# A windowed-attention stage: the mask in the scores' 64x64 tiling, and the weights' transposes, the values and the values' copy moved within a step

## The chip, the cores and the metric

The kernel runs on one core of a Trainium2 chip. The metric is device time in microseconds (us) for one execution. Before the change it is 1746.39 us, the median of 3 runs (1744.85 to 1749.19).

Five engines work side by side, each through its own instructions in order: PE (TensorE, the matrix unit; its weight loads are listed as PEld), DVE (VectorE), ACT (ScalarE), POOL (GpSimd) and SP (SyncE, here only a queue of transfers). They wait for each other by semaphores.

## The reference

Four stages run on 8 sequences of 512 tokens of 128 features, each followed by a layer norm. The change is in the last of them, two layers of windowed attention with a gated feed-forward part:

```
def _layer(x, wqkv, qs, ksc, wo, lg, lb, w1, b1, w2, b2):
    h = shift_token(x)                       # half of the features come from the token before
    q, k, v = split(h @ wqkv, 3)             # 8 heads of 64
    q = l2norm(q) * qs;  k = l2norm(k) * ksc
    q, k = rotary_xpos(q, k)
    # windows of 64 queries against 128 keys: their own window and the one before
    sim = einsum('bhwid,bhwjd->bhwij', q * 8, k)
    mask = (i < j) | (i > j + 64) | (j == -1)
    attn = softmax(where(mask, -max, sim))
    x = x + (attn @ v) @ wo
    h = layernorm(shift_token(x)) * lg + lb
    a, g = split(h @ w1 + b1, 2)
    return x + (a * gelu(g)) @ w2 + b2
```

`j == -1` holds for the missing window before a sequence's first.

## The kernel before

The earlier stages (attention with a distance bias, a feed-forward part with quantised operands, a second attention) take the first 1045 us or so: the last stage's scores run from 1046.4 to 1692.5 us of the profiled span, which ends at 1743.2.

The last stage goes through 16 items `k` (8 sequences in layer 0, then 8 in layer 1) of 4 chunks `c` of 128 tokens. A chunk holds two windows, `w` = 0 and 1, and 8 heads as 4 pairs `pr` with a half `s` each: `s` = 0 lies on partitions 0 to 63, `s` = 1 on 64 to 127. The program has a step for each chunk number `t` = 4k + c (the loop at line 1017), and works on several chunks in one step. Four steps make a **round**; c0 to c3 are its steps by the chunk t, so that the scores of a chunk c = 0 stand in step c2. In a step, in the order in which the lines stand:

- `begin` (PE, chunk t): the q and k projections into `q_ps` and `k_ps`, one PSUM bank each.
- `weights_T` (PE, chunk t-4): eight 128x128 transposes of the softmax weights `pw` into `p_ps`.
- `squares` of k (ACT) and `rotate` of q (DVE, two operations with outputs `was_k`, `was_q`).
- `over_sums` (chunk t-3): a reciprocal on DVE, then POOL divides `pw` by the sums.
- `weights_taken` (DVE, chunk t-4): two copies `pT<-p_ps`.
- `scores` (PE, chunk t-2): the mask, as a product of a bf16 selection matrix and a bf16 mask table, starts each of two PSUM banks `sp` (one for each `s`), and 16 products of 64 features, 64 queries and 128 keys are added to them. The pool of `sp` has one buffer for each half.
- `squares` of q (ACT; it follows `rotate` of q, as both read `q_ps`), `maxima` (DVE: two reductions of `sp`, and a small operation `m<-m,was_v`).
- In c3: `load_T` (PE transposes `hT`, ACT copies them). In c2: `turned` (PE transposes `nT` of an earlier item's normalised tokens), `turned_taken` (ACT copies `nT`), `v_of`, and `geglu`: six products `gp`, `ap`, three Gelu activations on ACT, three operations `u` on DVE. In c1: `normed` (DVE statistics of `hn`, POOL's small operations on them).
- `rotate` of k (DVE), `v_of` (PE: `v_ps`, ACT: a copy `v`, SP: two transfers into `ve`), `operands_T` (PE: eight transposes into `t_ps`), `operands` (ACT: copies `kT` and `qT`).
- `values` (PE, chunk t-4): 32 products of 64 columns, `o_ps<-pT,v` and `o_ps<-pT,ve`.
- `sizes` (DVE: a reduction `was_v<-was_k` and an addition; POOL: an addition).
- `weights` (ACT, chunk t-2): eight Exp activations `pw<-sp,m`, each with a read of its sum.
- `norms` (POOL: a maximum, a power of 2.93 us, a product `was_k<-was_k,was_v`).
- `values_taken` (ACT, chunk t-4): a copy `oT<-o_ps`. In c1 `normalized` (four ACT operations on `hn`) follows.
- `sums` (PE `y_ps`, DVE two additions into `xs`): output projection of chunk t-5 and second feed-forward product of chunk t-11.

Every engine executes in exactly this order of lines. Other than `q_ps`, `k_ps` and `sp`, products go to four PSUM banks in turn. Almost all instructions go through a helper at line 646, so the profile names line 646 for them; they are told apart by the tile.

The scores' mask before:

```
for s in range(2):
    r = slice(64 * s, 64 * s + 64)
    by, to = (twice[r], mask[r, 1]) if c else (identb, mask[:, 0])
    mm(sp[s], lhsT=by, rhs=to, start=True, stop=False, skip_group_check=True)
```

So for c = 0 it multiplies 128 rows by 128 columns, for the others 64 by 128, while the scores that follow use 64 by 64 and the values 128 by 64 parts of PE's array.

Of the kernel before, what the change touches and what calls it, by code (L numbers as in the profile page):

```python
# [11 lines left out]
BF16 = mybir.dt.bfloat16  # L12
I32 = mybir.dt.int32
AF = mybir.ActivationFunctionType
ALU = mybir.AluOpType
# [3 lines left out]
P = 128  # L19
# [6 lines left out]
C_ID, C_TRI, C_SEL, C_MASK0, C_MASK, C_ROT = 0, 128, 256, 512, 640, 768  # L26
# [25 lines left out]
def body(ctx, tc, x, consts, rows, wa0, wa1, acols, bo, wf, wqkv, wo, w1, w2, cols, b2r, qs, ks, out):  # L52
    nc = tc.nc
# [10 lines left out]
    sel = outer.tile([P, 2 * P], BF16, name="sel")  # L64
# [577 lines left out]
    def ffn1():  # L642
# [4 lines left out]
        mm, tr, act, copy = kept(nc.tensor.matmul), kept(nc.tensor.transpose), kept(nc.scalar.activation), kept(nc.scalar.copy)  # L647
# [53 lines left out]
        def shifted(src, h):  # L701

            p_set(h[0:1, 0, 64:128], 0.0)
            for at, n in ((0, 112), (112, 15)):
                nc.sync.dma_start(out=h[at + 1 : at + 1 + n, :, 64:128], in_=src[at : at + n, :, 64:128])
            nc.sync.dma_start(out=h[0:1, 1:NT, 64:128], in_=src[P - 1 : P, 0 : NT - 1, 64:128])
            nc.sync.dma_start(out=h[:, :, 0:64], in_=src[:, :, 0:64])
            return h

        def rows_of(k):  # L710
            return slice((k % B) * NT, (k % B + 1) * NT)
# [36 lines left out]
        def load(k):  # L748
            item[k]["h"] = shifted((xs if k >= B else xn)[:, rows_of(k), :], hq)
# [32 lines left out]
        def main():  # L782
            with ExitStack() as st:
                pool = lambda name, bufs, **k: st.enter_context(tc.tile_pool(name=f"l{name}", bufs=bufs, **k))
                const = pool("c", 1)
# [2 lines left out]
                tiles = lambda t: t.rearrange("p (c d) -> p c d", c=NT)  # L788
                identb = const.tile([P, P], BF16, name="identb")
                nc.vector.tensor_copy(identb, ident)  # L790
                twice = const.tile([P, P], BF16, name="twice")
                nc.vector.tensor_tensor(twice, sel[:, 0:P], sel[:, P : 2 * P], ALU.add)
                mask = const.tile([P, 2, 4, P], BF16, name="mask")
                for i, at in enumerate((C_MASK0, C_MASK)):
                    nc.vector.tensor_copy(mask[:, i], cst[:, at : at + P].unsqueeze(1).broadcast_to([P, 4, P]))
# [1 line left out]
                for i in range(2):  # L797
                    t = const.tile([P, 4, PAD + S], F32, name=f"kT{i}")
# [38 lines left out]
                def scores(k, c, h):  # L837


                    kT, qT = kTs[k % 2], h.pop("qT")  # L840
                    h["sp"] = sp = [p_s.tile([P, 4, P], F32, tag=f"s{s}", name="sp") for s in range(2)]
                    for s in range(2):
                        r = slice(64 * s, 64 * s + 64)
                        by, to = (twice[r], mask[r, 1]) if c else (identb, mask[:, 0])
                        mm(sp[s], lhsT=by, rhs=to, start=True, stop=False, skip_group_check=True)
                    for pr in range(4):
                        for s in range(2):
                            r = slice(64 * s, 64 * s + 64)
                            for w in range(2):
                                at = c * P + 64 * w  # L850
                                mm(
                                    sp[s][64 * w : 64 * w + 64, pr, :], lhsT=qT[r, pr, 64 * w : 64 * w + 64],
                                    rhs=kT[r, pr, at : at + P], start=False, stop=pr == 3 and w == 1, skip_group_check=True,
                                )
# [118 lines left out]
                def turned(k):  # L973
                    item[k]["nT_ps"], hn = bank("nT"), item[k].pop("hn")
                    for c in range(NT):
                        tr(item[k]["nT_ps"][:, c * P : (c + 1) * P], hn[:, c, :], ident)
# [26 lines left out]
                def load_T(k):  # L1003
                    item[k]["hT"] = transposed(item[k].pop("h"), "hT", 3)

                def at_(j, f, *a):
                    if 0 <= j < LAST:
                        f(*divmod(j, NT), chunk[j], *a)

                def begun(t, f, *a):  # L1010
                    if t >= EARLY:
                        at_(t, f, *a)
# [4 lines left out]
                for t in range(1, LAST):  # L1017
                    k, c = divmod(t, NT)
                    if c == 1 and k + 1 < K:
                        load(k + 1)  # L1020
                    begun(t, begin)
                    at_(t - 4, weights_T)
                    begun(t, squares, 1)
                    begun(t, rotate, 0)
                    at_(t - 3, over_sums)
                    at_(t - 4, weights_taken)
                    at_(t - 2, scores)
                    begun(t, squares, 0)
                    at_(t - 2, maxima)
                    if c == 3 and k + 1 < K:  # L1030
                        load_T(k + 1)
                    if c == 2 and 0 <= k - 2 < K:
                        turned(k - 2)
                        turned_taken(k - 2)
                        at_(t - 2, v_of)
                        geglu(k - 2)
                    if c == 1 and 0 <= k - 2 < K:
                        normed(k - 2)
                    begun(t, rotate, 1)
                    if not (c == 2 and 0 <= k - 2 < K):  # L1040
                        at_(t - 2, v_of)
                    at_(t - 1, operands_T)
                    at_(t - 1, operands)
                    at_(t - 4, values)
                    begun(t, sizes)
                    at_(t - 2, weights)
                    begun(t, norms)
                    at_(t - 4, values_taken)
                    if c == 1 and 0 <= k - 2 < K:
                        h = item[k - 2]["hn"]  # L1050
                        normalized(h, h, item[k - 2].pop("shape"))
                    sums(t - 5, t - 11)
                    if c == 0 and 0 <= k - 2 < K:
                        hn = work.tile([P, NT, D], F32, tag="hn", name="hn", bufs=1)
                        item[k - 2]["hn"] = shifted(xs[:, rows_of(k - 2), :], hn)
                    if t in (4, 5):
                        scaled_weights(t - 4)
                    if t == 6:
                        tables(1)
                    z = t - 11  # L1060
                    if z >= B * NT and z % NT == NT - 1:
                        item[z // NT]["shape"] = moments(xs[:, rows_of(z // NT), :], "f")
                    if z > B * NT and z % NT == 0:
                        finished(z // NT - 1 - B)
# [168 lines left out]
def _constants():  # L1233
    p, f = np.arange(P)[:, None], np.arange(P)[None, :]
    c = np.zeros((P, C_ALL), np.float32)
    c[:, C_ID : C_ID + P] = p == f
    i = p % 64
    c[:, C_TRI : C_TRI + 64] = -2.0 * np.maximum(f[:, 0:64] - i, 0)
    c[:, C_TRI + 64 : C_TRI + P] = -2.0 * np.maximum(i - f[:, 0:64], 0)
    for a in range(2):  # L1240
        c[:, C_SEL + a * P : C_SEL + (a + 1) * P] = f == 64 * a + i
    seen = (f >= i) & (f <= i + 64)
    c[:, C_MASK : C_MASK + P] = np.where(seen, 0.0, -1e30)
    c[:, C_MASK0 : C_MASK0 + P] = np.where(seen & ((p >= 64) | (f >= 64)), 0.0, -1e30)
    half = np.arange(0, DH, 2, dtype=np.float32)
    inv_freq = np.float32(1.0) / np.float32(10000.0) ** (half / np.float32(DH))
    t = np.arange(S, dtype=np.float32)
    freqs = (t[:, None] * inv_freq[None, :]).astype(np.float64)
    base = (half + np.float32(0.4 * DH)) / np.float32(1.4 * DH)
    power = (t - S // 2) / np.float32(32.0)  # L1250
    scale = base.astype(np.float64)[None, :] ** power.astype(np.float64)[:, None]
    cos, sin = np.cos(freqs), np.sin(freqs)
    for n, sc in enumerate((8.0 * scale, 1.0 / scale)):
        for k, (a, z) in enumerate(((cos, cos), (-sin, sin))):
            tab = np.concatenate([a * sc, z * sc], 1).reshape(NT, P, DH).transpose(1, 0, 2)
            at = C_ROT + (2 * n + k) * NT * DH
            c[:, at : at + NT * DH] = tab.reshape(P, NT * DH)

    at, blk = np.arange(S) - S // 2, np.arange(S) // 64
    rows = np.zeros((17, 2, S), np.float32)  # L1260
    for n in range(8):
        sign = np.where(blk <= n, 1.0, -1.0)
        rows[n, 0], rows[8 + n, 0] = blk == n, (blk == n) * at
        rows[n, 1], rows[8 + n, 1] = sign * at, -sign
    rows[16, 1] = -1.0
    return c, rows
# [55 lines left out]
```

## Time and profile before

| what | value |
|---|---|
| time, median of 3 runs | 1746.39 us (1744.85 to 1749.19) |
| profiled execution: span, first to last instruction | 1743.2 us |
| granted TensorE clock over the span | 0.972 |
| busy, share of the span: PE / DVE / ACT / POOL | 94% / 80% / 72% / 52% |
| a round of layer 0 (1309 to 1350), of 41 us: PE / DVE / ACT / POOL busy | 41.00 / 34.91 / 33.75 / 34.10 |
| a round of layer 1 (1599 to 1641), of 42 us: the same | 41.56 / 37.05 / 35.28 / 37.03 |
| one Exp of the last stage, mean, x512 | 479 ns |
| two pT copies, DVE, mean of one | 666 ns |

The median lies 3.2 us over the profiled span; a time is compared with the one, a row of the trace with the other. PE's spans in the trace contain the way through the array, so that one matmul's span overlaps the next: what it costs is read from the distance of two starts. The last stage's weight is in its rounds: FFN products (`gp`) begin in 14 steps of the loop, from 1121.8 us on, and the last two items' come after the loop.

### The profile page before, as it was taken

How to read it: one execution, taken by the hardware profiler on the slowest of the kernel's cores; microseconds unless marked ns; L12 is line 12 of the kernel's file. 1: busy time of each engine (PE TensorE's matmuls, PEld its weight loads, DVE VectorE, ACT ScalarE, POOL GpSimd, SP SyncE). 2: the span in 40 equal slices, each digit the busy share in tenths (PEclk: the TensorE clock that was granted, in tenths of full speed). 3: DMA queues.
4: the chain of work that ended last, by engine and by line, in shares of the span. 5: the costliest groups of instructions: out<-in, count | busy, mean ns of one | idle time of the engine just before them, and what ended most of it. 6: DMA issues, size and time to landing. Idle time of an engine off the chain costs nothing.

```text
span 1743.2 us, 42096 instructions
## 1 busy us (share of the span) xinstructions
PE 1638.7 (94%) x16305; PEld 947.9 (54%) x16305; DVE 1387.7 (80%) x2220; ACT 1257.6 (72%) x2996; POOL 911.8 (52%) x974
## 2 busy tenths in 40 slices
PE   3999999999988889999999988999999999999995
PEld 2454555455546644444444436566766676666664
DVE  4688777878839888888888857888888888888873
ACT  0577777777764558877777867788887888888883
POOL 3223332332125741323322157988888888888873
PEclk7899999999998979999999999999999999999998
DMA  6635222221110234233223101111111111111110
GB/s 133 143 72 142 65 54 47 68 58 26 14 14 1 62 78 81 64 63 74 67 49 59 42 4 35 35 35 37 41 38 35 35 41 37 43 42 42 37 35 25
DMA packets 92809, 90.27 MB, mean 52 GB/s; under 512 B 45969, under 2 KB 58257, under 8 KB 92610
## 3 DMA queue, kind: packets, MB, share of 16 engines
q1 hardware_dynamic: 87280, 85.52, 22.8%
q8 instruction: 130, 2.13, 0.5%
q10 hardware_dynamic: 1234, 1.52, 0.3%
q0 software_dynamic: 4096, 0.54, 0.2%
q14 instruction: 69, 0.57, 0.1%
HBM read 41.85 MB, written 18.87 MB: 35 GB/s over the span
## 4 chain that ended last, share of the span: by engine, by line
PE 75%; DVE 8%; ACT 6%; POOL 5%; issue 2%; DMA 2%; SPq 1%; DVEq 0%; ACTq 0%; POOLq 0%
PE av L259 15%; PE s_ps L259 12%; PE t_ps L259 9%; PE y_ps L646 5%; PE sp L646 4%; PE o_ps L646 3%; PE t_ps L646 3%; PE v_ps L646 3%; ACT e L48 2%; PE q_ps L646 2%; PE k_ps L646 2%; PE p_ps L646 2%; PE gp L646 2%; PE ap L646 2%; PE o_ps L260 2%
## 5 line engine op out<-in xcount | busy, mean ns | idle before, releaser
L48 DVE TENSOR_REDUCE m<-s_ps 128x2 f32<-128x1024 f32 x512 | 621.3, 1224 | 150.4 <-PE s_ps L259 146.1
L48 ACT ACTIVATE e<-t_ps 128x512 f32<-128x512 f32 x1024 | 556.1, 596 | 179.9 <-PE t_ps L259 173.1
L259 PE MATMUL av<-e,va 128*32 128x256 f32 x4096 | 328.3, 393 | 10.7 <-ACT avs L48 10.6
L259 PE MATMUL s_ps<-k,q 63*128 63x512 f32 x1024 | 263.1, 509 | 24.1 <-DMA q<-far 17.7
L48 POOL DMA_DIRECT2D q<-mt x128 | 68.9, 542 | 361.2 <-ACT mt L48 361.2
L259 PE MATMUL t_ps<-q,k 64*128 64x512 f32 x1024 | 247.6, 447 | 1.3 <-ACT e L48 1.3
L646 ACT ACTIVATE pw<-sp,m,was_v 128x128 f32<-128x128 f32 x512 | 227.3, 479 | 1.5 <-DVE m L646 1.0
L259 PEld LDWEIGHTS s_ps<-k,q 63*128 63x128 f32 x1024 | 98.6, 188 | 230.5 <-issue 154.0
L646 POOL TENSOR_TENSOR was_v<-was_v 128x16 f32<-128x16 f32 x64 | 187.5, 2930 | 5.3
L259 PEld LDWEIGHTS av<-e,va 128*32 128x32 f32 x4096 | 81.5, 108 | 100.8 <-issue 59.3
L259 PEld LDWEIGHTS t_ps<-q,k 64*128 64x128 f32 x1024 | 121.9, 189 | 23.3 <-ACT e L48 11.3
L646 POOL TENSOR_TENSOR pw<-pw,den 128x1024 f32<-128x1024 f32 x64 | 121.2, 1894 | 7.6 <-DVE den L646 7.6
L646 ACT ACTIVATION_READ_ACCUMULATOR pw<-sp,m,was_v 128x1 f32 x512 | 116.0, 227 | 0.0
L259 PEld LDWEIGHTS <-sel 64*128 64x128 bf16 x2048 | 66.5, 97 | 76.3 <-issue 53.5
L646 DVE TENSOR_REDUCE m<-sp 128x4 f32<-128x512 f32 x128 | 82.3, 684 | 18.9 <-PE sp L646 17.2
L646 POOL TENSOR_TENSOR was_k<-was_k,was_q 128x512 f32<-128x512 f32 x64 | 88.1, 1376 | 7.8 <-DVE was_q L646 7.8
L48 POOL CAST parts<-x 128x512 fp32r<-128x512 f32 x32 | 19.4, 607 | 135.9 <-ACT x L48 135.9
L646 ACT COPY v<-v_ps 128x512 f32<-128x512 f32 x64 | 37.6, 588 | 71.9 <-PE v_ps L646 71.9
L646 PEld LDWEIGHTS t_ps<-cst,was_k 128*128 128x128 f32 x512 | 59.6, 142 | 44.3 <-issue 22.6
L646 DVE COPY pT<-p_ps 128x512 f32<-128x512 f32 x128 | 79.9, 666 | 0.5 <-PE p_ps L646 0.5
L646 PEld LDWEIGHTS p_ps<-cst,pw 128*128 128x128 f32 x512 | 59.8, 141 | 32.3 <-issue 27.5
L646 DVE TENSOR_REDUCE was_v<-was_k 128x16 f32<-128x1024 f32 x64 | 77.1, 1205 | 0.0
(192 smaller groups left out, 3292.0 us busy)
## 6 DMA issues: line engine op xcount, KB each, us to landing
far<-parts SPq DMA_DIRECT2D x64, 256.0 KB
q<-far SPq DMA_DIRECT2D x256, 64.0 KB
k<-far SPq DMA_DIRECT2D x240, 64.0 KB
ve<-v SPq DMA_DIRECT2D x112, 128.0 KB
xn<-in_x SPq DMA_DIRECT2D x8, 256.0 KB
q<-mt POOLq DMA_DIRECT2D x128, 4.0 KB, 3.1
hn<-xs SPq DMA_DIRECT2D x16, 128.0 KB
hn<-xs SPq DMA_DIRECT2D x16, 112.0 KB
```

The costliest lines, as they stand in the source:

```text
L48: return lambda *a, **k: self.tc.keep_in_program_order(f(*a, **k))
L259: mm = lambda *a, **k: tc.keep_in_program_order(nc.tensor.matmul(*a, **k))
L260: tr = lambda *a, **k: tc.keep_in_program_order(nc.tensor.transpose(*a, **k))
L646: kept = lambda f: lambda *a, **k: tc.keep_in_program_order(f(*a, **k))
```

## The change

Five edits, all in the last stage:

1. The mask is written as four products of 64 by 64 (`s` by `w`), all with the bf16 identity `identb`; the matrix `twice` and the DVE operation that made it go, and the first window's mask table is used for `w` = 0 of c = 0 alone.
2. `weights_T` stands ahead of `begin`.
3. `weights_taken` stands ahead of `rotate` of q (and of `over_sums`).
4. `values` stands directly behind `scores`.
5. `values_taken` stands behind `squares` of q, ahead of `maxima`, `turned_taken`, `v_of`, `operands` and `weights`.

Steps after the loop (`rest`, line 1068) keep their order.

```diff
-                twice = const.tile([P, P], BF16, name="twice")
-                nc.vector.tensor_tensor(twice, sel[:, 0:P], sel[:, P : 2 * P], ALU.add)
...
-                    for s in range(2):
-                        r = slice(64 * s, 64 * s + 64)
-                        by, to = (twice[r], mask[r, 1]) if c else (identb, mask[:, 0])
-                        mm(sp[s], lhsT=by, rhs=to, start=True, stop=False, skip_group_check=True)
+                    for w in range(2):
+                        for s in range(2):
+                            r = slice(64 * s, 64 * s + 64)
+                            mm(
+                                sp[s][64 * w : 64 * w + 64], lhsT=identb[r, r], rhs=mask[r, 1 if c or w else 0],
+                                start=True, stop=False, skip_group_check=True,
+                            )
...
+                    at_(t - 4, weights_T)
                     begun(t, begin)
-                    at_(t - 4, weights_T)
                     begun(t, squares, 1)
+                    at_(t - 4, weights_taken)
                     begun(t, rotate, 0)
                     at_(t - 3, over_sums)
-                    at_(t - 4, weights_taken)
                     at_(t - 2, scores)
+                    at_(t - 4, values)
                     begun(t, squares, 0)
+                    at_(t - 4, values_taken)
                     at_(t - 2, maxima)
...
                     at_(t - 1, operands_T)
                     at_(t - 1, operands)
-                    at_(t - 4, values)
                     begun(t, sizes)
                     at_(t - 2, weights)
                     begun(t, norms)
-                    at_(t - 4, values_taken)
...
-    c[:, C_MASK0 : C_MASK0 + P] = np.where(seen & ((p >= 64) | (f >= 64)), 0.0, -1e30)
+    c[:, C_MASK0 : C_MASK0 + P] = np.where(seen & (f >= 64), 0.0, -1e30)
```

## The prediction

> **What bounds the kernel now.** I read the page's busy shares first, then stretches of the last stage, then the waits, and last the chain and three engines' timelines over a round. By the page and the stretches, PE is full.
>
> ```profile
> PE 1638.7 (94%) x16305; PEld 947.9 (54%) x16305; DVE 1387.7 (80%) x2220; ACT 1257.6 (72%) x2996; POOL 911.8 (52%) x974
> ```
> ```profile
> 1309.00:1350.00 41.00, 41.00 (x427) 28.15 (x423) 34.91 (x67) 33.75 (x99) 34.10 (x29) 1.00 0.17 37
> 1599.00:1641.00 42.00, 41.56 (x427) 28.09 (x428) 37.05 (x76) 35.28 (x104) 37.03 (x34) 1.00 0.15 36
> ```
>
> The columns are PE, PEld, DVE, ACT, POOL. A round of layer 0 has no gap on PE; one of layer 1 has, so something else paces it. The waits (1100 to 1680) name it:
>
> ```profile
> PEld gp L646 <- ACT nT L646: 11.2, 14, 1.1
> ...
> ACT was_k L646 <- DVE was_q L646: 4.3, 14, 0.5
> ```
>
> In c2 of each round PE's `gp` waits for ACT's copy `nT`, and ACT in turn for DVE's `rotate`. The chain in a round of layer 1 is not PE's there:
>
> ```profile
> 1573.47 1.58 DVE was_k L646
> 1575.05 0.40 DVE xs L646 x2
> 1575.45 0.60 DVE was_k L646
> 1576.05 0.61 DVE was_q L646
> 1576.83 0.40 issue
> 1577.23 0.59 ACT nT L646
> 1577.87 1.13 PE gp L646 x2
> ```
>
> How tight the same place is in layer 0: `gp` starts at 1328.25, just when PE is free of `v_ps`, and the `nT` copy ends at 1328.18 (1327.59 + 0.59): some 0.03 us spare after a semaphore. The three timelines there:
>
> ```profile
> 1325.71 0.68 DVE L646 TENSOR_TENSOR was_k<-q_ps,was_q 128x512 f32<-128x512 f32 x1
> 1326.31 0.68 DVE L646 TENSOR_TENSOR was_q<-q_ps,was_q 128x512 f32<-128x512 f32 x1
> 1326.90 0.19 DVE L646 RECIPROCAL den<-den 128x8 f32<-128x8 f32 x1
> 1327.01 1.24 DVE L646 COPY pT<-p_ps 128x512 f32<-128x512 f32 x2
> 1328.17 1.28 DVE L646 TENSOR_REDUCE m<-sp 128x4 f32<-128x512 f32 x2
> ```
> ```profile
> 1324.16 0.64 ACT L646 COPY oT<-o_ps 128x512 f32<-128x512 f32 x1
> 1324.62 1.71 ACT L646 ACTIVATE hn<-hn,mr,rstd 128x128 f32<-128x128 f32 x4
> 1326.17 0.64 ACT L646 ACTIVATE was_k<-k_ps 128x512 f32<-128x512 f32 x1
> 1327.08 0.60 ACT L646 ACTIVATE was_k<-q_ps 128x512 f32<-128x512 f32 x1 [0.26 <-DVE was_q L646]
> 1327.59 0.59 ACT L646 COPY nT<-nT 128x512 f32<-128x512 f32 x1
> ```
> ```profile
> 1309.39 1.90 POOL L646 TENSOR_TENSOR pw<-pw,den 128x1024 f32<-128x1024 f32 x1
> ...
> 1318.61 1.89 POOL L646 TENSOR_TENSOR pw<-pw,den 128x1024 f32<-128x1024 f32 x1
> ```
>
> **The loop.** DVE's small `m` ends 0.02 us after POOL's `pw` wherever the two overlap (1302.26 after 1302.24; 1311.31 after 1311.28; 1320.52 after 1320.49), and takes 0.45 to 0.96 us instead of 0.17. From `m` follow `rotate` of k, the reduction, POOL's power and product, and the next `pw`. So a round is a closed path: from `rotate` of k in c2 (1293.14) to `m` of c3 9.12 us, to `m` of c0 9.04, to `m` of c1 9.22 (1320.52), then statistics, `rotate`, reduction and additions until DVE is free in c2, 5.19 (1325.71), then `rotate` of q, ACT's `squares`, `nT`, `gp` 2.54 (1328.25), then PE's six products and DVE's `u` to `rotate` of k 6.17 (1334.42). Sum 41.28: the round of PE. In layer 1 POOL's row is longer by 1.0, and the round is 42.26: there this loop alone paces.
>
> **The change part by part.** *Mask and values on PE.* Starts in c0: last transpose of `p_ps` 1307.79, mask 1308.00, first score 1308.32, second group 1308.48, then every 0.11. A change of tiling thus costs 0.1 over the streaming (0.21 for 512 columns). With the mask in the scores' tiling 0.11 goes and most of 0.05 (first loads not fetched ahead); the new mask's own loads cost 0 to 0.05, the nearest row being the scores' first group. I take 0.13. A 64x64 bf16 mask is in no row: four scores' products start within 0.02 us and run together, two bf16 masks of 64x128 too, so I take the four as together, 0.21; if they went by pairs 0.43, one by one 0.85. In c2 two masks of 128 rows went in turn (1325.34 to the first score at 1325.86): 0.34 goes behind the first mask, and a drain of 0.1 now stands ahead of it, 0.24. *Values behind scores*: the way from `t_ps` into `o_ps` (0.20 instead of 0.11) and out to `y_ps` (0.16 instead of 0.06, then 0.21 instead of 0.11) goes, and the drain behind the scores is there already: 0.20. PE alone: 0.33 in c0, c1, c3, 0.44 in c2, 1.43 a round.
>
> *What the scores' banks make of it.* The second mask waits for the last Exp of the step before; `o_ps` now lies in this path. Before: mask 1308.00 to `v_ps` 1310.48, three copies and eight Exps to 1315.60, 0.05 to a next mask: 7.65, hidden in a step of 8.72. Now `o_ps` with its drain (1.08) less 0.13 comes in: 8.60 in c0 and c1; c3 with `hT` (0.39) 8.99; c2: mask to the end of `t_ps` 9.02 (1325.34 to 1334.36) plus 1.08 less 0.34, then the table load and Exps to the mask at 1340.19, 5.83: 15.59. Sum 41.78, more than the 41.28 of now: this alone takes all of PE's gain.
>
> *`weights_taken` ahead of `rotate` of q.* In c2 DVE is the late one, free at 1325.71 only while `q_ps` is long done. Two copies, 1.15 us (1327.01 to 1328.17), now precede `rotate`, ACT's `squares` and `nT`: the loop grows by 1.15. In the other steps DVE waits before `maxima` (0.50 for the scores in c0), which covers the move. *`values_taken` ahead of `nT`*: `oT` takes 0.46 of ACT (1324.16 to 1324.62) between `squares` and `nT`: 0.46 more. In c0, c1, c3 it lies in ACT's wait for `v_ps` (2.16 us before 1310.52). `o_ps` waits for `pT` too, some 0.7 us in c2, but is free before ACT is.
>
> *Hidden.* `weights_T` 1.7 us sooner: its `pw` is done at 1311.28 and needed at 1314.0, where the q projection starts now. Banks: its second one waits for the `qT` copy, done at 1312.07, needed at 1314.5. `ve` transfers are issued at 1311.1 to 1312.3 and used two steps on, some 15 us. POOL's and SP's orders stay; no DMA moves. `twice` goes before the stage, 0.1 or less. Tail: 0 to 0.9 more, `o_ps` in one last pass, nothing taken.
>
> **Two rules of the Trainium skill against this.** DVE's copies of `pT` ran beside POOL operations with SBUF inputs (1576.68, during an addition to 1577.43) in 0.63 us, unblocked; `m` was blocked. The page "SBUF — State Buffer", "Who interferes with whom", lets a DVE copy in a two-port mode, and any DVE operation with two SBUF inputs, be locked out by GpSimd. [...] "TensorEngine Tiling (Array Packing)", "Restrictions", says that column tiling switches fast weight load off, so the new mask's loads are slower; no row here shows such a load; the sum, which the loop sets, would stay.
>
> **Sum.** 1.15 + 0.46 = 1.61 a round: 42.9 in layer 0, 43.9 in layer 1; both exceed 41.78, so the banks' path stays hidden. 14 rounds of the loop hold `gp`: 14 x 1.61 = 22.5, less 9 x 0.03 spare, is 22. On the profiled span, 1743.2 to 1765; on the runs, which lie 3.2 above, 1746.4 to 1768.5.
>
> **Rivals.** *PE paces alone* (the other side): then a round loses 1.43 and the wait of 0.30 that c3's second mask has now (1339.89 to 1340.19), 39.55: 9 x 1.73 + 5 x 2.71 = 29, about 1717. For it: PE's 41.00 of 41.00 and the chain of layer 0. Against: `gp` has 0.03 spare, and the scores' banks have one buffer. It decides only if the loop had over 1.6 of room and the last Exp came 0.2 (c0) to 1.6 (c2) sooner. *The banks alone pace*: DVE takes the copies in idle time; layer 0 9 x 0.5 more, layer 1 5 x 0.5 less: 2 more, 1748.5, no change. Against: DVE idles nowhere between 1319.57 and 1328.8. *Half of the shift*: ACT or DVE hides one move: 14 x 0.46 to 14 x 1.15, 1753 to 1763. *The masks do not run together*: one by one adds 0.64 a step to the banks' path, 44.3 a round: 3.0 x 9 + 2.1 x 5 = 37, 1784; by pairs 42.6, hidden. *The change does not do what it says* (a drain remains ahead of the scores): 0.16 a step, 42.4 a round on the banks' path, hidden: the forecast's time.
>
> **How the numbers follow.** Forecast 0.70, half of the shift 0.12, masks apart 0.08, banks alone 0.05, PE alone 0.05. The forecast's own spread is 1761 to 1776 (a tail of 0.9, 0.5 either way a round). The range 1753 to 1784 takes in half of the shift and masks apart and leaves out the two rivals of 0.05. Within 0.3% (5.2 us; finer a measurement of this kernel can't tell) lie the banks alone and a shift that is smaller yet: 0.06; faster 0.05; slower 0.89.
>
> **What would show it.** Rounds of 42.9 and 43.9 instead of 41.28 and 42.26; in c2 `gp` waits for ACT's `nT` some 0.4 us, and `o_ps` for DVE's `pT` 0.7 in layer 0 and 1.5 or so in layer 1; masks wait for ACT's `pw`, mostly in c3, 1.6 where before it was 0.30; the step from mask to first score falls from 0.32 to between 0.21 and 0.26. Wrong I am if rounds get shorter, if `gp` follows `v_ps` at once, or if `m` no longer ends with `pw`.

## The result, and the profile after

| kernel | median, us | lowest to highest | ratio to before, 95% interval |
|---|---|---|---|
| before | 1745.91 | 1744.85 to 1749.19 (4 runs) | |
| after | 1763.12 | 1758.02 to 1765.72 (4 runs) | 1.0096 [1.0078, 1.0113] |

The change costs 17.2 us on the medians. The profiled execution of the changed kernel lies 19.9 above that of before: span 1763.1 against 1743.2, clock 0.970 against 0.972. Forecast were 22 more and 1768.5.

The page's busy shares and the same two stretches of the last stage as before (PE, PEld, DVE, ACT, POOL, then the clock):

```profile
PE 1633.9 (93%) x16433; PEld 958.8 (54%) x16433; DVE 1382.8 (78%) x2219; ACT 1263.1 (72%) x2996; POOL 912.1 (52%) x974
```
```profile
1309.00:1350.00 41.00, 39.23 (x430) 27.94 (x430) 33.68 (x64) 32.25 (x92) 33.06 (x27) 1.00 0.17 37
1599.00:1641.00 42.00, 40.57 (x437) 28.78 (x436) 35.13 (x75) 35.77 (x104) 36.96 (x34) 1.00 0.18 43
```

PE was full in layer 0 (41.00 of 41.00). Now 1.8 us of the stretch are empty, and every other engine does less in that stretch too: the same work lies in a longer round. In layer 1 PE has only 1.0 less than before. What PE waits for, between 1100 and 1680:

```profile
ACT was_k L646 <- DVE was_q L646: 21.9, 27, 1.5
...
PE sp L646 <- ACT pw L646: 16.8, 16, 1.4
PEld gp L646 <- ACT nT L646: 13.2, 13, 1.1
...
PEld o_ps L646 <- DVE pT L646: 7.1, 18, 0.6
```

The row of `sp` was 0.6 us before, in one wait; now it is 16.8 in 16. The row of ACT behind `rotate` of q went from 4.3 to 21.9. The chain through c2 of a round in layer 0:

```profile
1337.76 1.20 DVE pT L646 x2
1338.95 0.60 DVE was_k L646
1339.55 0.61 DVE was_q L646
1340.16 0.02 issue
1340.18 0.02 ACTq L646
1340.20 0.04 issue
1340.24 0.58 ACT was_k L646
1340.82 0.38 issue
1341.20 0.61 ACT nT L646
1341.82 0.04 issue
1341.86 1.12 PE gp L646 x2
```

The two moved copies stand in the chain ahead of `rotate`. The 0.38 called issue between `squares` and `nT` is the other moved piece, `oT`, as ACT's own timeline shows:

```profile
1340.24 0.60 ACT L646 ACTIVATE was_k<-q_ps 128x512 f32<-128x512 f32 x1 [1.23 <-DVE was_q L646]
1340.74 0.58 ACT L646 COPY oT<-o_ps 128x512 f32<-128x512 f32 x1
1341.20 0.60 ACT L646 COPY nT<-nT 128x512 f32<-128x512 f32 x1
```

From the starts of `gp`, the whole difference of the two profiled executions can be told round by round:

| stretch | before | after | difference | forecast |
|---|---|---|---|---|
| to the last stage's first mask | 1045.39 | 1046.30 | +0.9 | 0 |
| first mask to first `gp` | 76.43 | 78.80 | +2.4 | +1.6 |
| second round | 41.30 | 44.75 | +3.4 | +1.6 |
| 7 rounds of layer 0, mean | 41.28 | 42.98 | +11.9 | +11.3 |
| the round between the layers | 41.29 | 42.95 | +1.7 | +1.6 |
| 4 rounds of layer 1, mean | 42.27 | 41.90 | -1.5 | +6.4 |
| last of these `gp` to the end | 80.74 | 81.82 | +1.1 | 0 to 0.9 |

So layer 0 is what was forecast (42.94 to 42.96 in six of the seven rounds), layer 1 went the other way, and the start lost more. The first and the last row are no effect of a step that can be named: over the 14 profiled executions of this study the first mask starts anywhere from 1043.6 to 1048.0, and the tail takes 80.4 to 83.7.

### The profile page after: what moved, and what is told of

Same layout as the page of the kernel before. It is cut to its first block, busy times and chain, and to the rows that moved or that the text cites. A ratio compares the mean times of both kernels' runs of the same rounds, so it can differ in the third digit from the quotient of the medians.

```text
span 1763.1 us, 42324 instructions
## 1 busy us (share of the span) xinstructions
PE 1633.9 (93%) x16433; PEld 958.8 (54%) x16433; DVE 1382.8 (78%) x2219; ACT 1263.1 (72%) x2996; POOL 912.1 (52%) x974
## 4 chain that ended last, share of the span: by engine, by line
PE 68%; DVE 11%; ACT 8%; POOL 5%; issue 3%; DMA 3%; SPq 1%; DVEq 0%; ACTq 0%; POOLq 0%
PE av L259 15%; PE s_ps L259 12%; PE t_ps L259 9%; PE y_ps L646 4%; PE sp L646 3%; PE gp L646 2%; ACT e L48 2%; DVE was_k L646 2%; PE ap L646 2%; ACT pw L646 2%; PE o_ps L646 2%; PE o_ps L260 2%; PE p_ps L646 2%; PE t_ps L646 2%; PE q_ps L646 2%
## 5 line engine op out<-in xcount | busy, mean ns | idle before, releaser
L646 DVE SCALAR_TENSOR_TENSOR u<-ap,cols_s,u 128x512 f32<-128x512 f32 (+3 forms) x51 | 36.6, 717 | 67.2 <-ACT u L646 35.5
L646 PE MATMUL sp<-kT,qT 64*64 64x128 f32 x2048 | 80.3, 271 | 0.5 <-ACT qT L646 0.5
L646 PE MATMUL o_ps<-pT,ve 128*64 128x64 f32 x1024 | 71.4, 230 | 6.5 <-DVE pT L646 5.9
```

The source lines that it names most:

```text
L646: kept = lambda f: lambda *a, **k: tc.keep_in_program_order(f(*a, **k))
```

## The experiments

Unless said otherwise a round is the distance of two `gp` groups in the profiled execution. All ratios are to the kernel before, timed beside the run.

### Which move costs what

**1. `over_sums` behind `maxima`**, in the changed kernel, so that POOL's `pw` can't start before `m` is done.

```diff
-                    at_(t - 3, over_sums)
                     at_(t - 2, scores)
...
                     at_(t - 2, maxima)
+                    at_(t - 3, over_sums)
```

> The changed kernel with over_sums (DVE's reciprocal, POOL's division pw) placed behind maxima instead of ahead of scores, so that DVE's m no longer stands behind POOL's pw. Theory A (in layer 0 the loop of DVE, POOL and ACT sets the round of 42.95, because m ends with pw): m takes 0.17 us in every step, the loop opens, and every round falls to the path through the scores' banks, 41.78: 8 rounds of layer 0 by 1.17, some 9 us less than the changed kernel, about 1754. Rival B (what costs is DVE's amount of work in c2, or PE's waits for the moved copies): rounds stay at 42.9, 1763. Rival C (PE's own work sets the pace once m is free): rounds of 39.6 to 41.0, below 1746.

Measured: 1757.70 us (1753.32 to 1761.97), ratio 1.0066 [1.0048, 1.0083]. `m` takes 0.17 us in every step of the rounds. Four of seven rounds of layer 0 are 41.77, the banks' path, the other three 43.2 to 43.8; layer 1 has 41.75 in three of four. So the loop went through `m`, and behind it the banks stand at 41.77. The long rounds have a new limit: DVE's statistics wait for the transfer of `hn` (`DVE bn <- DMA hn<-xs`, 7.8 us in 5 waits). The later `pw` moves the blocking: POOL's product `was_k<-was_k,was_q` behind it now runs beside `rotate`'s last operation on k, of the same name on DVE, which takes 1.62 us instead of 0.68 (from 1322.63, while POOL's runs from 1322.43 to 1323.69). So the additions into `xs`, which the transfer reads, come later.

**2. `weights_taken` behind `rotate` of q again**, all else as changed.

```diff
-                    at_(t - 4, weights_taken)
                     begun(t, rotate, 0)
                     at_(t - 3, over_sums)
+                    at_(t - 4, weights_taken)
```

> The changed kernel with weights_taken back behind rotate of q and over_sums. Theory A (the longest way from DVE's end of c1 to gp counts): now o_ps waits for pT, which ends 2.56 us after DVE is free, and nT, v_ps follow on PE: gp 5.0 us after DVE is free instead of 4.2, so rounds of layer 0 grow by 0.8 to 0.9, 7 us more, about 1770; layer 1 the same or up to 0.3 a round more. Rival B (the copies' 1.15 us ahead of rotate is the cost, whatever stands where): rounds of layer 0 fall by 1.15 to 41.8, about 1754.

Measured: 1782.05 us (1779.20 to 1782.90), ratio 1.0200 [1.0184, 1.0217]: undoing this edit makes it worse. Layer 0 has 43.76, as the first theory had it. Layer 1, which that theory left within 0.3 us, has 44.7 to 44.8 in three of four rounds: `m` of c1 starts 0.37 us behind `pw` there and takes 1.55, so that the loop is closed again. Experiment 9 shows the reason for layer 0 without the other edits.

**3. `values_taken` behind `turned_taken`** in the steps c2 that have `geglu`, so that ACT copies `nT` first.

```diff
                     begun(t, squares, 0)
-                    at_(t - 4, values_taken)
+                    if not (c == 2 and 0 <= k - 2 < K):
+                        at_(t - 4, values_taken)
                     at_(t - 2, maxima)
...
                         turned_taken(k - 2)
+                        at_(t - 4, values_taken)
```

> The changed kernel, in the steps c2 with geglu alone values_taken placed behind turned_taken, so that ACT copies nT before oT. Theory A (ACT's oT lies in the loop with 0.46 us): gp then waits for PE's own v_ps, 0.42 us sooner: layer 0 42.5 a round, 8 times 0.42, 3.4 us less, about 1760; layer 1 unchanged. Rival B (the banks' path alone sets the round, or oT is hidden): no change, 1763.

Measured: 1757.28 us (1749.61 to 1760.09), ratio 1.0058 [1.0038, 1.0077]. Layer 0 has 42.50, 0.45 less than the changed kernel (the term was 0.46), layer 1 41.75. The copy of `oT` is a link of layer 0's loop. Its size is read from the changed kernel, 0.46 us from the start of `oT` to that of `nT` (1340.74 and 1341.20); that the round falls by just as much doesn't measure it, since another limit comes in: `gp` now starts the moment PE is done with `v_ps` (1339.40), which stands behind `o_ps` and its wait for `pT`.

**4. The mask edit alone** on the kernel before (edit 1 of the change, no move of a line).

> The kernel before with the mask's edit alone (four products of 64 by 64, all else in the old order). Theory A (the loop of DVE, POOL and ACT has 0.03 us spare in layer 0 and sets layer 1): PE saves 0.13 in c0, c1, c3 and 0.34 in c2, but the round stays at 41.26 and 42.26: 0 to 1 us less, 1745 to 1746, and gp waits for nT in layer 0 too. Rival B (PE paces layer 0): 9 rounds of 0.6 less, about 1740. Rival C (the four masks don't run together): the first score comes 0.43 or more after the mask and rounds get longer by up to 2.5.

Measured: 1746.08 us (1743.30 to 1748.08), ratio 0.9994 [0.9984, 1.0005]. Rounds of layer 0 are 41.26 in seven of nine (the others 41.31 and 41.45), those of layer 1 42.22 to 42.31, as before. PE is ready for `gp` 0.62 us before it starts (1324.80, two products of 0.43 after 1323.94, against 1325.42), as `nT` is late:

```profile
1323.94 1.02 PE L646 MATMUL v_ps<-wqkv_s,hT 128*128 128x512 f32 x2
1325.42 1.13 PE L646 MATMUL gp<-nT,w_s 128*128 128x512 f32 x2 [0.46 <-ACT nT L646]
```

PE's gain turns into a wait, since the loop has the same length. That is the plainest proof that PE, with no gap in a round, was not alone in setting it.

**5. `values` and `values_taken` in their old places**, with the mask, `weights_T` and `weights_taken` as changed.

> The changed kernel with values behind operands and values_taken behind norms again, as before; the mask, the weights' transposes and the copies pT stay changed. If the loop is the cause in layer 0: its 41.26 with the mask alone plus the two copies of 1.15 gives rounds of 42.4 (0.46 of oT and the o_ps part of the banks' path go). Layer 1 tells the theories apart: if the longer banks' path (o_ps in it) is what moves DVE's m ahead of POOL's pw in layer 1, m is blocked again there and the rounds are 43.4, in all 1762; if m escapes for another reason, rounds of 41.8 there, in all 1755. c3's second mask waits under 0.5 us instead of 1.57 in either case.

Measured: 1764.13 us (1759.04 to 1766.15), ratio 1.0115 [1.0099, 1.0130]; the profiled execution, 1759.04, is the fastest of its four, with clock 0.975. Layer 0 has 42.45, and layer 1 43.43: both forecast sizes, 1.2 over the mask alone. So the copies `pT` cost 1.2 in both layers, and in layer 1 of the changed kernel the place of `values` hides it. The two kernels differ there by 0.28 us in the order of two starts in step c1. First the changed kernel, DVE and then POOL:

```profile
1586.52 1.23 DVE L646 TENSOR_REDUCE m<-sp 128x4 f32<-128x512 f32 x2
1587.85 0.17 DVE L646 SCALAR_TENSOR_TENSOR m<-m,was_v 128x8 f32<-128x8 f32 x1
```
```profile
1586.90 1.04 POOL L646 TENSOR_TENSOR was_k<-was_k,was_v 128x512 f32<-128x512 f32 x1
...
1588.08 1.89 POOL L646 TENSOR_TENSOR pw<-pw,den 128x1024 f32<-128x1024 f32 x1
```

Then this run, DVE and POOL:

```profile
1577.60 1.29 DVE L646 TENSOR_REDUCE m<-sp 128x4 f32<-128x512 f32 x2
1578.99 1.86 DVE L646 SCALAR_TENSOR_TENSOR m<-m,was_v 128x8 f32<-128x8 f32 x1
```
```profile
1577.76 1.04 POOL L646 TENSOR_TENSOR was_k<-was_k,was_v 128x512 f32<-128x512 f32 x1
...
1578.94 1.89 POOL L646 TENSOR_TENSOR pw<-pw,den 128x1024 f32<-128x1024 f32 x1
```

With `values` behind the scores `m` starts 0.23 us ahead of `pw` and takes 0.17. With `values` in the old place it starts 0.05 behind and takes 1.86. In layer 1 the loop is closed only where the second order holds in c1. The place of `values` alone does not bring the first: it stands behind `scores` in experiments 2, 6 and 9 too, and there `m` of c1 takes 1.5 to 1.9 us in layer 1, with rounds of 43.0 to 46.2.

**6. `weights_T` behind `begin` again**, all else as changed.

```diff
-                    at_(t - 4, weights_T)
                     begun(t, begin)
+                    at_(t - 4, weights_T)
```

> The changed kernel with weights_T behind begin again, all else as changed. It prices edit 2, which was put at nothing. If the start of the stage lost because p_ps now stands ahead of the projections and waits there for POOL's table products and pw: the first gp comes 1.6 to 1.7 us sooner than in the changed kernel, no stretch at half clock lies at 1097, and the second round loses its 3.4: 1758 to 1761. If the half clock comes from the rest of the order, the first gp moves by 0.5 or less and the time stays at 1763. Rounds of layer 0 stay at 42.95 in both, and those of layer 1 at 41.8.

Measured: 1777.53 us (1775.22 to 1779.61), ratio 1.0188 [1.0172, 1.0203], slower than the change, which neither theory had. The first `gp` comes 3.4 us sooner (1121.68 against 1125.10), but 2.3 of these lie ahead of the first mask; from there it is 1.1. No half clock lies at 1097, yet the second round is still 1.5 longer than the next. And the rounds are 43.62 and 43.0 to 43.9: DVE's copies, now ahead of `rotate`, wait for transposes that come 1.7 us later. The waits of this run (1100 to 1680), a row that the changed kernel has only in its first steps:

```profile
DVE pT L646 <- PE p_ps L646: 32.5, 35, 1.7
```

So edit 2 is not merely free, it is what edit 3 stands on. I had priced each edit from the changed kernel's waits and not asked which one feeds the other.

**7. `over_sums` behind `maxima` on the kernel before**, with the diff of experiment 1.

> The kernel before with one move: over_sums (reciprocal on DVE, product pw on POOL) behind maxima instead of ahead of scores, so that m no longer runs beside pw. If the closed path DVE, POOL, ACT through m paces layer 1 and PE paces layer 0: m takes 0.17 us in every step, rounds of layer 0 stay at 41.2 to 41.3 and rounds of layer 1 fall from 42.26 to 41.3, 5 x 0.95 less, so 1741. Rival, the later pw delays what follows it (statistics of hn, whose transfer then comes late, as it did in the changed kernel with this move): rounds of 41.8 to 43 in layer 0 and 1750 or more.

Measured: 1746.83 us (1743.75 to 1750.79), ratio 1.0005 [0.9993, 1.0016]. `m` takes 0.17 everywhere; layer 1 falls from 42.27 to 41.58, but layer 0 rises from 41.28 to 41.56. In its chain `rotate`'s last operation on k is long again (1.62 in two steps of a round, as in experiment 1), and then PE waits for POOL's product (`POOL was_v 2.92`, `POOL was_k 1.05`, then `PE t_ps`): the later `pw` pushes POOL's chain back. The time lies between the two theories: the move gives with `m` and takes with `rotate` and POOL.

### Towards a faster order

**8. The mask edit with `over_sums` behind `maxima`**, in every step, in c1 alone, in c0 and c1, and mixed. The diff for c1 alone, on top of the mask edit:

```diff
-                    at_(t - 3, over_sums)
+                    if c != 1:
+                        at_(t - 3, over_sums)
...
                     at_(t - 2, maxima)
+                    if c == 1:
+                        at_(t - 3, over_sums)
```

In every step:

> The kernel before with the mask edit and over_sums behind maxima. With the mask edit alone PE was ready 0.62 us before nT, so that PE's own round is 40.65. If only the loop through m keeps PE from using that, rounds of 40.65 in both layers: 9 x 0.6 + 5 x 1.6 = 13.4 less than before, 1732 to 1734. Rival, the transfer of hn is the next limit: rounds of 41.8 to 43 in layer 0, 1746 to 1755. Between them, when m is free but another link of DVE's order holds nT: rounds of 41.0 to 41.3, 1737 to 1742.

In c1 alone:

> The kernel before with the mask edit and over_sums behind maxima in step c1 alone, where m is blocked longest (1.36 us in layer 0, 1.86 in layer 1). If m in c1 is the link that counts: layer 0 from 41.26 to PE's own 40.65, layer 1 from 42.25 to 40.65 to 41.1, and hn's transfer, issued in c0, is not late: 1732 to 1736. Rival, the late pw holds POOL's chain for t_ps and costs PE what m gains: 41.1 in both layers as with the move in every step, 1740.

In c0 and c1:

> As the run with the move in step c1 alone, but in c0 and c1. If layer 1 needs m free in both steps (1.68 and 1.86 there), it gives 40.7 to 41.1 in layer 1 where the move in c1 alone gives more; in layer 0 the later xs in c0 brings back the late transfer of hn, 41.1: 1736 to 1740. Rival: as the move in c1 alone, within 0.1 a round.

In c1, and from step 44 on in c0 too:

> The kernel before with the mask edit; over_sums behind maxima in c1 of every round and, from step 44 on (where POOL's row is longer), in c0 too. If the rounds of the two runs before simply combine: 40.62 in layer 0 as with c1 alone, 41.09 in layer 1 as with c0 and c1, 5 x 0.47 less than with c1 alone, so 1736. Rival: the change of order between the layers costs what it gains, 1738 to 1739.

| `pw` late in | median, us | range | ratio, 95% interval | layer 0 | layer 1 |
|---|---|---|---|---|---|
| every step | 1739.86 | 1736.08 to 1744.37 | 0.9972 [0.9960, 0.9984] | 41.05 to 41.74 | 41.08 |
| c1 | 1738.40 | 1736.91 to 1739.78 | 0.9952 [0.9935, 0.9969] | 40.62 to 40.64 (one 41.48) | 41.56 |
| c0 and c1 | 1740.13 | 1735.08 to 1740.99 | 0.9957 [0.9939, 0.9976] | 41.05 to 41.6 | 41.09 |
| c1, c0 from step 44 | 1738.11 | 1736.04 to 1740.73 | 0.9951 [0.9936, 0.9966] | 40.62 to 40.65, three 41.1 to 41.64 | 41.10 |

With `m` free in c1 alone, PE's mask gain comes through: 40.62 in layer 0, 0.66 less than before, close to the forecast's mask term (3 x 0.13 + 0.24 = 0.63), and the chain through such a round (1327.35 to 1367.97) is PE's alone. The step of a mask in c0 in the run with c1 alone, on PE:

```profile
1307.63 0.41 PE L646 MATMUL sp<-mask,identb 64*64 64x512 bf16 x4
1307.87 1.04 PE L646 MATMUL sp<-kT,qT 64*64 64x128 f32 x32
1308.84 1.12 PE L646 MATMUL v_ps<-wqkv_s,hT 128*128 128x512 f32 x2
```

Four masks in 0.24, then the scores at once; from this mask to the next is 8.575 us, where it was 8.72. Layer 1 of this run falls to 41.56 only, so that it misses its 1732 to 1736: `m` of c0 still takes 1.68 there. In the kernel with the move in every step the price shows: DVE's `m` is free, but `rotate`'s operation in c0 takes 1.62 (0.68 in every step of these rounds with the move in c1 alone), and `hn` comes late. Its chain, ahead of a round of 41.33:

```profile
1314.32 0.41 DVE xs L646 x2
1314.73 0.49 SPq L705
1315.21 0.05 issue
1315.27 0.96 SPq L705
1316.22 0.05 issue
1316.27 3.76 DMA hn<-xs
...
1320.16 0.87 DVE bn L646 x4
```

The four are not told apart by their times. All are 0.3 to 0.5% faster than the kernel before, with intervals below 1; the mixed one shows 41.10 in layer 1 as expected, yet three rounds of 41.1 to 41.64 in its earlier part, and its time is that of c1 alone, as the rival had it.

**9. Mask and `values` directly behind `scores`**, no other edit.

> The kernel before with the mask edit and values directly behind scores, and no other edit: weights' transposes, the copies pT and the copy oT stay in their old places. Theory of the forecast's closed paths: the banks' path with o_ps in it is 41.78, the loop with the mask alone is 41.26 to 41.28, so 41.8 in layer 0, 41.8 or 42.25 in layer 1, about 1750. Rival, from the run with the pT copies behind rotate: o_ps now stands ahead of the nT transposes, v_ps and gp on PE and waits in c2 for pT, which DVE makes behind rotate of q, so that gp is late by PE's order: its 43.76 less the 0.46 of oT is 43.3 in layer 0 and 44.3 in layer 1, with the long second round 1775 to 1780. In both, PE idles early in the stage and a stretch at half clock lies between 1095 and 1145.

Measured: 1783.08 us (1781.35 to 1789.81), ratio 1.0216 [1.0187, 1.0244], the slowest of all. Layer 0 has 44.05, layer 1 44.4 to 46.2: the rival, by 0.7 to 0.9 more than its sizes (45.2 is the mean of layer 1). Its chain in c2 says what `values` needs:

```profile
1338.45 0.60 DVE was_k L646
1339.05 0.60 DVE was_q L646
1339.64 0.11 DVE den L646
1339.75 1.17 DVE pT L646 x2
1340.92 0.04 issue
1340.96 1.15 PE o_ps L646 x30
1342.11 0.59 PE nT L646 x4
1342.69 0.86 PE v_ps L646 x2
1343.55 0.94 PE gp L646 x2
```

`o_ps` waits for DVE's copies, and behind it on PE stand the `nT` transposes, `v_ps` and `gp`, which do not need it. Here `nT` is no longer late by DVE and ACT but by PE's own order. In the changed kernel the copies come first, so that this wait is small (longest 0.6) and DVE's `rotate` is late in its place. Edits 2, 3 and 4 hang together; of the orders tried here the cheapest was to take none of the three.

## Why the prediction was right, and where it was wrong

**The loop in layer 0: right, in kind and size.** 42.9 was forecast and 42.95 is there. Taken apart: 41.26 with the mask alone, 42.45 with the copies `pT` (a term of 1.15, measured 1.19), 42.50 with everything but `oT` ahead of `nT` (0.46, in the trace 0.46). `gp` waits 0.42 us (PE ready 1341.44, start 1341.86), 0.4 in the text. The six stretches of the path had to add up to the round, as those of any path through a repeating trace do; what shows the loop is experiment 4, where PE's gain became a wait. The Trainium skill's page "SBUF — State Buffer", "Who interferes with whom", lets a DVE copy be locked out by GpSimd in a two-port mode. These copies out of PSUM were not: the two take 1.27 us from 1337.68 on, while POOL's `was_k<-was_k,was_q` runs from 1336.78 to 1338.50.

**The banks' path: right to a few hundredths.** Forecast from one mask to the next: 8.99 behind c3, 8.60, 8.60, and 15.59 through c2. Taken from the second masks of a round in layer 1: 8.99, 8.60, 8.60, 15.57, in all 41.76 against 41.78. In c3 the second mask waits 1.57 us behind the first (forecast 1.6):

```profile
1565.79 0.40 PE L646 MATMUL sp<-mask,identb 64*64 64x512 bf16 x1
1567.36 0.41 PE L646 MATMUL sp<-mask,identb 64*64 64x512 bf16 x3 [1.17 <-ACT pw L646]
```

In c0, c1 and c2 it waits 0.22, out of a gain on PE that was put at 0.33 (0.44 in c2), and the step falls from 8.72 to 8.60 only; before, it waited 0.003 in c0 and c1.

**Layer 1: the step that failed is "43.9 in layer 1; both exceed 41.78, so the banks' path stays hidden".** The rounds are 41.78, 41.76, 42.27 (there DVE's statistics wait 1.1 us for the transfer of `hn`) and 41.78. The 1.61 was laid on a loop that closes only while `m` starts behind `pw`, and I took "wherever the two overlap" as if they always overlapped. They did not even before: in layer 1 `m` of c3 started 0.61 us ahead of `pw` and took 0.17. The changed order let `m` of c1 start 0.23 us ahead (experiment 5), the loop fell open, and the next closed path, the banks', set the round. With `values` in the old place the loop stays closed and layer 1 is 43.43; so it does with `values` behind `scores` but `weights_T` or `weights_taken` late (experiments 2, 6 and 9). I had named the sign ("if `m` no longer ends with `pw`") but given it no price: four rounds of about 2, some 8 us. With it the sum would have been 14 instead of 22. How the order comes about is seen in the starts only (`pw` comes 3.35 us after the step's first mask in the changed kernel, 2.67 with the old place; `m` 3.12 and 2.72); which wait makes the 0.68 was not followed further.

**"Hidden" edits: nearly right in the rounds, wrong at the start.** From the first mask to the first `gp` 2.4 instead of 1.6 was lost, and the second round is 1.8 longer than those after it. Part of the first (experiment 6, without it, takes 1.1 less): `p_ps` now stands ahead of the projections and at 1095 waits 3.1 us for `pw`, which POOL reaches only behind its six table products (1092.62 to 1096.16). Before, the same `pw` ended at 1098.82 and only the transposes waited. But this alone does not cost the stretch its time: experiment 5 has the same order of `weights_T` and 76.31 from first mask to first `gp`. Nor does a half clock: experiment 2 has none there and takes 78.79. The loss goes with `values` behind `scores`: the six kernels that have it take 77.7 to 79.4, the eight others 75.3 to 77.2. Which wait makes it was not followed.

The second round goes with the clock. The stretch 1118 to 1145 in the changed kernel, in experiment 9 and in experiment 5:

```profile
1118.00:1145.00 27.00, 24.45 (x221) 16.37 (x220) 19.72 (x33) 20.93 (x58) 21.31 (x18) 0.94 0.10 22
```
```profile
1118.00:1145.00 27.00, 24.50 (x201) 15.93 (x205) 17.60 (x32) 19.04 (x52) 18.92 (x14) 0.94 0.13 30
```
```profile
1118.00:1145.00 27.00, 24.66 (x235) 15.89 (x236) 20.80 (x37) 20.80 (x56) 21.89 (x16) 1.00 0.14 31
```

The same six kernels show 0.94 there, the eight others 1.00. In five of the six the half clock begins within the second round (1134.6 to 1138.1), and that round is 1.5 to 2.6 longer than the mean of those that follow. In experiment 9 it lies mostly ahead of the first `gp` (1120.3 to 1123.8), and the second round is 0.2 longer. In the changed kernel PE had just idled 0.41 and 1.39 us for the banks (the masks at 1135.28 and 1137.04), and the values behind them took 1.90 instead of 1.08. All half-clock stretches of a profile begin a whole multiple of 3.41 us apart. Here are the step of that grid ahead of the half clock at 1138.09, and one in a later round with c3's wait:

```profile
1134.68:1138.09 3.41, 1.61 (x37) 1.24 (x36) 2.41 (x5) 3.29 (x14) 3.33 (x2) 1.00 0.00 0
```
```profile
1564.76:1568.17 3.41, 2.24 (x32) 1.10 (x34) 3.41 (x14) 3.04 (x13) 3.29 (x2) 1.00 0.00 0
```

PE idles 1.80 us in the first, 1.17 in the second, and only the first is followed by half clock. So the two waits of the second round, close together, empty more of such a step than the one of c3 in a later round, which is 1.57 from mask to mask but 1.17 of idle time. That the waits bring the half clock is still an inference, as no run changes them alone.

**Masks together: right.** In experiments 4 and 8 the four start within 0.01 us in three steps of four, and the first score comes 0.24 us after them (0.21 to 0.26 forecast). The new loads, which might have been slower, take 0.10 us each, side by side, and the step from the last transpose of `p_ps` to the mask is 0.20 where it was 0.21. In the changed kernel the first mask starts alone and the others 0.22 later, when the second bank is free, so that its 0.24 from the first mask to the first score is that wait. **PE alone paces** did not happen, and could not have: with the mask alone it was the loop (experiment 4), with `values` the banks. Its mask part is real (experiment 8); its part from `values`, 0.20 a step, shows nowhere by itself, as each kernel that has it is held by `o_ps` in the banks' path or by `pT`.

In sum: direction and mechanism right, layer 0's two terms right to 0.04 us. In layer 1 8 us too many were forecast. Some 3 too few at the start, and 2 us ahead of the first mask and behind the last round, which no step of the change explains, make up for over half of that in the profiled execution (22 against 19.9): that the total comes so near is luck.

## What to carry to other kernels

A round can have no gap on one engine and still be held by a closed path through others: take a little work away from the full engine (experiment 4) and see whether the round or only a wait moves. Add a moved step's price only to a path that stays closed: where two starts of different engines lie within a few tenths of a microsecond and their order decides whether one blocks the other, forecast both orders, each with the next path behind it. And price edits that feed each other together: copies moved ahead want their transposes ahead, and products moved ahead want the copies ahead, or they wait at the head of an engine's queue with others behind them. Where an operation is moved so that it no longer blocks another, ask which one it, or what follows it, blocks in the new place (experiments 1, 7 and 8).

## What was not expected of the hardware

- An operation of 0.17 us on DVE became one of 1.86 us by starting 0.05 us after POOL's product instead of 0.23 before it. A start 0.02 us ahead was not enough: in experiment 9 `m` of c1 takes 1.94 so. Ordering the two the other way in one step of four is worth 0.6 us a round with the new mask (40.62 against 41.26).
- Executions of one kernel vary with the granted clock: the changed kernel's four took 1765.18, 1758.02, 1765.72 and 1761.06 us at 0.970, 0.973, 0.971 and 0.972. A difference of 0.003 of 1760 us is 5.3 us, an estimate that covers most of the 7.2 between the first two. The stretches at half clock lie in other places from one profile to the next, also ahead of the last stage.
- In the last stage's rounds and the stretch before them, the granted clock fell to half for 6.8 us (from 1097.1) and 3.4 us (from 1138.1) in the changed kernel's profile. The Trainium skill's page "TensorE: Matmul & The Clock Gate", Part 1, has half rate follow an idle window of some 3.4 us. PE did work in the 3.41 us ahead of each of the two: it idled 2.13 us of the first and 1.80 of the second. How much is enough no run shows sharply: 1.72 us came ahead of the half clock in experiment 9 (1116.93 to 1120.34), while 1.76 us in experiment 5 (1631.26 to 1634.68) brought none.
